# A second level of block products in the second matrix product of a fused block, with its sums on GpSimd and all steps in a table

## The chip, the core and the metric

One NeuronCore of a Trainium2 chip runs the whole program. The metric is device time in microseconds of one execution, as the median of several runs. The engines are TensorE (PE in the profile; PEld is its load of stationary operands), VectorE (DVE), ScalarE (ACT), GpSimd (POOL) and SyncE (SP), which here only issues DMAs.

## The reference

32 sequences of 128 tokens with 512 features go through a conditioned block in float32:

```python
m = mask[:, :, None]
shift, scale, gate_msa = jnp.split(silu(t) @ ada_w + ada_b, 3, axis=1)
norm = jnp.where(m, layernorm(x) * (1 + scale[:, None]) + shift[:, None], 0)
fwd, bwd = two MLPs of width 512 with exact gelu on norm
x = x + gate_msa[:, None] * jnp.where(m, fwd + bwd, 0)
shift_mlp, scale_mlp, gate_mlp = jnp.split(silu(t) @ ffada_w + ffada_b, 3, axis=1)
ff_norm = layernorm(x) * (1 + scale_mlp[:, None]) + shift_mlp[:, None]
h = gelu(ff_norm @ ff_w1 + ff_b1, approximate=True)     # 512 -> 1024
return x + gate_mlp[:, None] * (h @ ff_w2 + ff_b2)      # 1024 -> 512
```

Few tokens are masked in, so the first half is small; what fills the time is the second half: for every token a first product (512 to 1024) and a second one (1024 to 512).

## The kernel before

The first 82 us do the masked tokens and the opening. Then four pairs follow (p = 0 to 3), each of two sides of four sequences, 1024 tokens. A pair's two sides are the two row blocks of a block product after Strassen and Winograd: seven products of half size instead of eight, with sums of blocks before and after.

The first product (FirstProduct) applies this twice, with seven streams of seven phases; one phase is four records of TensorE of 256 columns. Results gather in two PSUM banks, e and a, are copied or added into the hidden tiles ha and hb, and pass through gelu on ScalarE. Sums of hidden blocks run on GpSimd.

The second product (SecondProduct) applies it once. The list ORDER names fourteen steps: products P1 to P7, each for U (the first 256 columns of tokens of both sides) and V (the rest). `step` issues a step: two tiles of 128 tokens, four matmuls each of 256 output columns, with the tokens as stationary operand (`of_batch` takes every second float) and weights of `fw2` or sums of them in `t_2` as moving operand. Each of U and V has its own banks e and a. P3, P7 and P4 come last. After P5 ScalarE keeps a copy p5 of e and seeds e again; VectorE forms sums of hidden blocks (L1266, L1276, L1283, L1341); after a product that completes a block of results, `finish` multiplies it by the gate into a tile t (L1293) and adds that to x (L1295), both on VectorE, and `store` writes x out. The last half step of the last pair goes to two banks of its own (`last`), with a gate, an addition and a store for each.

Beside the second product, the next pair is prepared: its x is normalised and turned in blocks on VectorE (L945, L1490), moved between tiles by 32 DMAs, 24 from SyncE's queue and 8 from ScalarE's (L972), scaled in place by 32 activations on ScalarE (L955), and summed into token blocks s1, s2 and s4 by four VectorE operations (L1002). The loop over `step` puts these in between by hand-written places (`put`). All engines run in the order in which the code records the instructions; nothing is reordered, and an instruction waits for those it depends on.

## Time and profile before

| | us |
|---|---|
| median of 3 runs | 453.68 |
| the runs | 453.67 to 453.86 |
| the profiled execution | 453.94 |
| its span | 452.2 |
| TensorE busy, of the span | 444.6 |
| VectorE, ScalarE, GpSimd busy | 334.8, 179.0, 158.3 |
| span behind the last matmul | 4.65 |

A row of instructions names line, engine, operation, tiles written and read, and their size; then busy time, mean duration in ns, and the idle time of the engine ahead of it with what ended it. One matmul of the code leaves two records on TensorE. A record's mean duration contains its way through the pipeline (379 ns at 256 columns), so the pace is read from rows of the chain or the timeline: length over count. PEclk is the granted clock of TensorE, full from the opening on.

### The profile page before, as it was taken

What the parts mean: (1) busy time and instruction counts of PE and PEld (TensorE: products, weight loads), DVE (VectorE), ACT (ScalarE), POOL (GpSimd) and SP (SyncE); (2) the same over time, 40 slices, a digit from 0 to 9 for tenths busy, and PEclk for the clock granted to TensorE, in tenths of its full rate; (3) what the DMA queues carried; (4) which work ended last, traced back from release to release, by engine and by line L of the source; (5) the groups of instructions that cost most, each with busy time, mean ns of one, the idle gap of its engine ahead of it and who ended that gap; (6) DMA issues with size and microseconds to landing.
All of it is one profiled execution on the core that took longest, in us unless ns stands there. A gap on an engine that the chain in (4) does not pass through costs nothing.

```text
span 452.2 us, 6204 instructions
## 1 busy us (share of the span) xinstructions
PE 444.6 (98%) x2147; PEld 376.1 (83%) x2147; DVE 334.8 (74%) x573; ACT 179.0 (40%) x389; POOL 158.3 (35%) x154
## 2 busy tenths in 40 slices
PE   8999999999999999999999999999999999999995
PEld 3884585688898998888899988888999888899995
DVE  5798798877699677977895779878956785434645
ACT  3124127253651831546528315464274244642000
POOL 4211460089760000797600007977000027560000
PEclk9999999999999999999999999999999999999998
DMA  7999439847335517741275176412751434122022
GB/s 249 375 399 408 171 72 331 290 152 251 107 138 143 93 49 268 234 138 36 94 189 92 46 267 230 141 38 92 187 95 46 175 128 128 36 93 95 0 94 96
DMA packets 56768, 70.84 MB, mean 157 GB/s; under 512 B 34724, under 2 KB 35836, under 8 KB 55710
## 3 DMA queue, kind: packets, MB, share of 16 engines
q1 hardware_dynamic: 43790, 57.76, 39.2%
q0 software_dynamic: 4160, 10.54, 6.6%
q10 hardware_dynamic: 8784, 2.11, 2.5%
q8 instruction: 18, 0.29, 0.2%
q14 instruction: 16, 0.13, 0.1%
HBM read 56.71 MB, written 13.70 MB: 156 GB/s over the span
## 4 chain that ended last, share of the span: by engine, by line
PE 88%; DVE 5%; issue 2%; POOL 2%; DMA 1%; ACT 1%; POOLq 0%; DVEq 0%
PE a_o L1319 21%; PE a_m L1132 20%; PE e_o L1319 16%; PE e_m L1132 15%; PE po_s L222 6%; PE ph_s L681 2%; PE ph_s L205 2%; DVE xn L945 1%; DVE xn L1490 1%; PE pm_ss L308 1%; PE last L1319 1%; PE a_m_alone L1132 1%; DMA x_wide<-t_s 1%; DMA x<-x_wide,slot_i 1%; PE pm_f L308 1%
## 5 line engine op out<-in xcount | busy, mean ns | idle before, releaser
L1183 POOL TENSOR_TENSOR ha<-p_m,ha 128x512 f32<-128x512 f32 x20 | 25.9, 1293 | 176.3 <-ACT ha L1190 166.4
L1319 PE MATMUL e_o<-fw,ha 128*128 128x256 f32 x256 | 57.9, 379 | 1.0 <-DVE ha L1341 1.0
L1319 PEld LDWEIGHTS e_o<-fw,ha 128*128 128x128 f32 x256 | 50.2, 196 | 6.3 <-issue 1.3
L955 ACT ACTIVATE xT<-xT,modT 128x128 f32<-128x128 f32 x112 | 45.0, 496 | 23.9 <-DMA xT<-xn 22.3
L1319 PE MATMUL a_o<-t,hb 128*128 128x256 f32 x240 | 54.1, 379 | 0.0
L1319 PEld LDWEIGHTS a_o<-t,hb 128*128 128x128 f32 x240 | 47.1, 196 | 4.7
L1094 ACT ACTIVATE hb<-hb,biasT 128x256 f32<-128x256 f32 x64 | 29.0, 500 | 28.3 <-POOL hb L1216 16.1
L1146 ACT COPY p_m<-e_m 128x512 f32<-128x512 f32 x27 | 15.9, 587 | 56.4 <-PE e_m L1132 56.4
L901 POOL DMA_INDIRECT x<-x_rows,slot_i x24 | 27.3, 1136 | 6.2 <-issue 5.4
L1183 POOL TENSOR_TENSOR hb<-p_m,hb 128x512 f32<-128x512 f32 x20 | 29.2, 1461 | 0.3
L1319 PE MATMUL e_o<-fw,s 128*128 128x256 f32 x128 | 28.9, 379 | 0.0
L1319 PE MATMUL a_o<-fw,ha 128*128 128x256 f32 x128 | 28.9, 379 | 0.0
L1319 PE MATMUL a_o<-t,s 128*128 128x256 f32 x128 | 28.9, 379 | 0.0
L222 PE MATMUL po_s<-w,h_s 128*128 128x512 f32 x64 | 28.4, 594 | 0.0
L1190 ACT COPY ha<-e_m 128x512 f32<-128x512 f32 x32 | 18.5, 580 | 24.8 <-PE e_m L1132 24.4
L1319 PEld LDWEIGHTS a_o<-fw,ha 128*128 128x128 f32 x128 | 25.1, 196 | 2.5
L1319 PEld LDWEIGHTS e_o<-fw,s 128*128 128x128 f32 x128 | 25.1, 196 | 2.5
L1319 PEld LDWEIGHTS a_o<-t,s 128*128 128x128 f32 x128 | 25.1, 196 | 2.5
L1157 DVE TENSOR_TENSOR e_m<-a_m,ha 128x512 f32<-128x512 f32 x20 | 13.9, 697 | 17.0 <-POOL ha L1183 7.6
L1094 ACT ACTIVATE ha<-e_m,biasT 128x256 f32<-128x256 f32 x48 | 20.1, 469 | 14.4 <-PE e_m L1132 14.4
L1132 PE MATMUL a_m<-xT,tw 128*128 128x256 f32 x96 | 24.7, 380 | 0.0
L1132 PE MATMUL e_m<-s,fw 128*128 128x256 f32 x92 | 23.7, 380 | 0.0
(234 smaller groups left out, 894.7 us busy)
## 6 DMA issues: line engine op xcount, KB each, us to landing
x<-in_x_dram SPq DMA_DIRECT2D x16, 512.0 KB, 7.5
tw<-t_rows SPq DMA_DIRECT2D x16, 512.0 KB, 4.0
gate<-gate_rows POOLq DMA_DIRECT2D x8, 1024.0 KB, 4.9
out_dram<-x SPq DMA_DIRECT2D x15, 512.0 KB, 4.5
tw<-t_rows SPq DMA_DIRECT2D x16, 384.0 KB, 3.6
xT<-xn SPq DMA_DIRECT2D x80, 64.0 KB, 2.2
ada_f<-in_L_cond_ffada_w_dram SPq DMA_DIRECT2D x4, 768.0 KB, 14.9
ada_a<-in_L_cond_ada_w_dram SPq DMA_DIRECT2D x4, 512.0 KB, 3.5
```

Source lines behind the costliest of these rows:

```text
L205: nc.tensor.matmul(ph[:, :n], w[:, k, ts(f, P)], xT[:, k, :], start=(k == 0), stop=(k == KC - 1))
L222: nc.tensor.matmul(po, h[f][:, ts(i, P)], w[:, f, :], start=(f == 0 and seeded is None), stop=(f == HC - 1), skip_group_check=seeded is no ...
L308: nc.tensor.matmul(pm[ts(j, B), : (hi - lo) * P], sT[:, k, :], kinds[:, k, lo:hi, ts(j, P)], start=(k == 0 and not begun), stop=True, skip ...
L901: nc.gpsimd.indirect_dma_start(out=xs[i // G][i % G // 2][:, i % 2], out_offset=None, in_=x1_rows, in_offset=bass.IndirectOffsetOnAxis(ap= ...
L955: nc.scalar.activation(out, src, AF.Identity, bias=shift, scale=scale)
L1094: nc.scalar.activation(dst[:, n], src[:, n], AF.Gelu_apprx_tanh, bias=biasT[:, f : f + 1])
L1132: nc.tensor.matmul(bank[:, ts(n, QT)], self.w_block(j, product)[:, ts(n, P)], self.x_block(j, product), start=(product in ("P1", "P5") and ...
L1146: nc.scalar.copy(p5, e)
L1157: nc.vector.tensor_tensor(e, a, p5, add)
L1183: nc.gpsimd.tensor_tensor(self.place(RESULT[j], c), self.p5[j], other, ALU.add)
L1190: nc.scalar.copy(self.place(RESULT[j], c), src)
L1319: nc.tensor.matmul(part, of_batch(src[:, k], i), w[product][:, k, :], start=(last and k == 0), stop=True, skip_group_check=True,)
```

## The change

The three products P3, P7 and P4 of each second product are no longer done as two steps each, U and V. Each is divided once more (class Inner): seven inner products p1 to p7 of 256 tokens by 256 hidden features by 128 columns. p1, p6 and p7 share one bank (`one`), p5 has another (`five`); ScalarE copies p5, p1 and p7 into a tile d (C in the table), VectorE adds d's part to the bank after p6 and p7 (V), and then adds d to the outer bank (join, J). p2, p3 and p4 go straight into the outer banks. The four sums of token blocks of each (S1 to S4) run on GpSimd. The seven blocks of weights of each product come from `fw2`, `t_2` and twelve sums made by VectorE in pair 0, kept in quarters of the first product's weights that are no longer read and in a small new tile.

Four of the eight results of a pair (both blocks of side 0) are copied out of PSUM by ScalarE and multiplied by the gate and added to x by GpSimd; the other four are multiplied on VectorE in place in PSUM and added. The third block result of P7 is formed in e in place of a tile. The normalising of side 1 moves to ScalarE, with a small operation for its bias. The 32 moves are single steps. And every step of the loop has a name, and a table (ORDER) gives for each pair the sequence of all steps, first product and preparation included.

```diff
+    INNER = ("P3", "P7", "P4")
...
+            if by_vector:
+                nc.vector.tensor_scalar(
+                    t, src, self.mv[:, i, 0:1], self.rstd[:, i : i + 1], ALU.subtract, ALU.mult
+                )
+            else:
+                nc.scalar.activation(
+                    t, src, AF.Identity, bias=self.lift[:, i : i + 1], scale=self.rstd[:, i : i + 1]
+                )
...
-            nc.vector.tensor_tensor(t, view, gate, ALU.mult)
+            nc.vector.tensor_tensor(view, view, gate, ALU.mult)
...
+        def kept(self, c, side, h, n):
+            t = tp.tile([P, 512], F32, tag="t", name=f"t_{self.p}_{c}{side}{h}")
+            self.own[c, side, h] = t
+            nc.scalar.copy(t, self.banks[c][n])
...
+            nc.gpsimd.tensor_tensor(view, view, self.gate[side][:, 2 * c : 2 * c + 2, part], ALU.mult)
...
+            nc.gpsimd.tensor_tensor(xt, view, xt, ALU.add)
...
+        def direct(self, product, q):
+
+            c, n = {"p2": (0, 0), "p3": (0, 1), "p4": (1, 0)}[q]
+            bank = bank_of(product, self.banks[c])
+            out = bank.rearrange("p (i f) -> p i f", i=2)[:, :, ts(n, P)]
+            self.inner[product].multiply(q, out, False)
+
+        def join(self, product, c):
+
+            bank = bank_of(product, self.banks[c]).rearrange("p (i f) -> p i f", i=2)
+            nc.vector.tensor_tensor(bank, bank, self.inner[product].d[:, c], ALU.add)
...
+    class Inner:
...
+        def sum(self, j):
+            if j < 3:
+                self.s[j] = self.second.s_of(self.product, j - 1)
+            (a11, a12), (a21, a22) = self.x
+            s1, s2 = self.s.get(1), self.s.get(2)
+            out, x, y, op = {
+                1: (s1, a21, a22, ALU.add),
+                2: (s2, s1, a11, ALU.subtract),
+                3: (a21, a11, a21, ALU.subtract),
+                4: (a11, a12, s2, ALU.subtract),
+            }[j]
+            nc.gpsimd.tensor_tensor(out, x, y, op)
+
+        def multiply(self, q, out, start, tiles=range(2)):
...
+            w = inner_w[self.product][q]
+            for i in tiles:
+                for k in range(2):
                     nc.tensor.matmul(
-                        part,
+                        out[:, i % out.shape[1]],
                         of_batch(src[:, k], i),
-                        w[product][:, k, :],
-                        start=(last and k == 0),
+                        w[:, k, :],
+                        start=(start and (i == 0 or out.shape[1] == 1) and k == 0),
                         stop=True,
                         skip_group_check=True,
                     )
...
+        def copy(self, q):
+
+            if self.d is None:
+                self.d = self.second.d_of(self.product)
+            c, n, which = {"p5": (1, 1, "five"), "p1": (0, 0, "one"), "p7": (1, 0, "one")}[q]
+            nc.scalar.copy(self.d[:, c, :, ts(n, P)], self.view(which))
+
+        def with_five(self, c):
+
+            five = self.d[:, 1, :, P:]
+            nc.vector.tensor_tensor(self.d[:, c, :, P:], self.view("one"), five, ALU.add)
...
+            c030 4i3 lg1 c010 c031 6i7 c011 V6i7 S4i7 R001 c013
+            n1P1 7i7 K010 J70 3i7 A2 V7i7 2i7 E20 S1i4 5i4 S3i4 C7i7 C5i4 1i4 J71 c023 A3 G110 n1P5
...
+        steps.run(ORDER.get(p, "").split())
```

In the table 6i7 is p6 of P7, V6i7 the addition behind it, S1i4 the sum S1 of P4, C a copy, c a scaling, K, G and R the copy, gate and addition of a result, J a join, A a sum of token blocks, E the third block result, n1P1 a phase of the next pair's first product.

TensorE in pair 1, from P2 of V on. Before, with e and a the banks of U (0) and V (1):

```order
L1319 MATMUL e_o_1_1789<-fw_312,ha_1432 128x256 x8
L1319 MATMUL a_o_1_1790<-t_314,s_1_1505 128x256 x8
L1319 MATMUL e_o_0_1731<-fw_312,ha_1432 128x256 x8
L1319 MATMUL a_o_0_1732<-t_314,hb_1433 128x256 x8
L1319 MATMUL e_o_1_1789<-fw_312,ha_1432 128x256 x8
L1319 MATMUL a_o_1_1790<-t_314,hb_1433 128x256 x8
L1132 MATMUL e_m_1_2023<-s_2_1974,fw_311 128x256 x2
```

And of the change, from the first half of P6 of V on, where one and five are the banks of the inner products and si the sums that GpSimd makes:

```order
L1384 MATMUL a_o_1_1834<-t_314,s_1_1852 128x256 x4
L1470 MATMUL five_P_2033<-fw_312,si_1_P_2024 128x128 x4
L1470 MATMUL one_P_2043<-fw_312,ha_1558 128x128 x4
L1384 MATMUL a_o_1_1834<-t_314,s_1_1852 128x256 x4
L1470 MATMUL one_P_2043<-inner_more,si_1_P_2027 128x128 x4
L1470 MATMUL five_P_2066<-t_314,si_1_P_2048 128x128 x4
L1470 MATMUL one_P_2043<-inner_more,ha_1558 128x128 x4
L1470 MATMUL e_o_0_1800<-fw_312,ha_1558 128x128 x4
L1470 MATMUL one_P_2097<-t_314,hb_1559 128x128 x4
...
L1470 MATMUL e_o_1_1833<-t_313,ha_1558 128x128 x4
L1470 MATMUL one_P_2097<-t_313,si_1_P_2072 128x128 x4
```

Where six steps of eight matmuls stood, inner products of four stand, P3's (one_P_2043) and P7's (one_P_2097) side by side; between the uses of one bank lies one other product, or two.

GpSimd at the same place in pair 1, where before it had no work. L1459 is a sum S, L1346 a gate, L1353 an addition to x:

```order
L1459 TENSOR_TENSOR si_1_P_2024<-ha_1558 128x512
L1459 TENSOR_TENSOR ha_1558<-ha_1558 128x2x256
L1459 TENSOR_TENSOR si_1_P_2027<-si_1_P_2024,ha_1558 128x512
L1459 TENSOR_TENSOR si_1_P_2048<-hb_1559 128x512
L1459 TENSOR_TENSOR ha_1558<-ha_1558,si_1_P_2027 128x2x256
L1459 TENSOR_TENSOR si_1_P_2072<-si_1_P_2048,hb_1559 128x512
L1459 TENSOR_TENSOR hb_1559<-hb_1559 128x2x256
L1346 TENSOR_TENSOR t_100_2021<-t_100_2021,gate_0_1878 128x512
L912 DMA gate_1_2116<-gate_rows 128x2048
L1459 TENSOR_TENSOR hb_1559<-hb_1559,si_1_P_2072 128x2x256
L1353 TENSOR_TENSOR x_1_387<-t_100_2021,x_1_387 128x2x256
L1459 TENSOR_TENSOR si_1_P_2151<-hb_1559 128x512
```

The last row is S1 of P4, the eleventh operation of the engine from P3's S1 on, apart from the gate's issue.

VectorE at the end of the last pair, from P4's p6 on (before, the rows there were four gates and additions and those of `last`). L1502 is V, L1417 a join, L1328 a gate, L1335 an addition, L1425 and L1427 those of `last`:

```order
L1395 TENSOR_TENSOR e_o_1_3110<-a_o_1_3111,p_o_1_3182 128x512
L1328 TENSOR_TENSOR e_o_1_3110<-e_o_1_3110,gate_1_3159 128x512
L1502 TENSOR_TENSOR xn_d_3223<-one_P_3314,xn_d_3223 128x2x128
L1417 TENSOR_TENSOR a_o_0_3077<-a_o_0_3077,xn_d_3223 128x512
L1335 TENSOR_TENSOR x_2316<-e_o_1_3110,x_2316 128x2x256
L1502 TENSOR_TENSOR xn_d_3223<-one_P_3314,xn_d_3223 128x2x128
L1417 TENSOR_TENSOR a_o_1_3111<-a_o_1_3111,xn_d_3223 128x512
L1328 TENSOR_TENSOR a_o_1_3111<-a_o_1_3111,gate_1_3159 128x512
L1328 TENSOR_TENSOR a_o_0_3077<-a_o_0_3077,gate_1_3159 128x512
L1335 TENSOR_TENSOR x_2316<-a_o_1_3111,x_2316 128x2x256
L1335 TENSOR_TENSOR x_2314<-a_o_0_3077,x_2314 128x2x256
L1425 TENSOR_TENSOR last_3371<-last_3371,gate_1_3159 128x128
```

Both V and both joins of P4 stand among the last gates and additions, and the rows of `last` are behind all of them.

More of the change, by code (lines that the diff above doesn't have):

```diff
@@ new lines @@
+        put("E1", second.third, 1)
+        sums("P7")
+        apart("P3", "p7")
+        join("P3", 1)
+        put_scales(1)
+        apart("P7", "p5", "p1")
+        direct("P3", "p2")
+        apart("P7", "p6")
+        join("P7", 0)
+        direct("P3", "p3")
+        second.finish(put, 0, 0, 1, 0)
+        put("o00", second.store, 0, 0)
+        apart("P7", "p7")
+        join("P7", 1)
+        sums("P4")
+        direct("P3", "p4")
+        second.finish(put, 1, 0, 1, 0)
+        put("o10", second.store, 1, 0)
```

829 lines of the change are left out of this document (551 added, 278 removed).

## The prediction

> **What bounds the kernel now.** I read the page's busy shares and chain first, then the windows by stage, then the waits of TensorE.
>
> ```profile
> PE 444.6 (98%) x2147; PEld 376.1 (83%) x2147; DVE 334.8 (74%) x573; ACT 179.0 (40%) x389; POOL 158.3 (35%) x154
> PE 88%; DVE 5%; issue 2%; POOL 2%; DMA 1%; ACT 1%; POOLq 0%; DVEq 0%
> ...
> 82.60:168.08 85.48, 84.50 (x390) 74.66 (x389) 68.47 (x106) 41.46 (x91) 35.91 (x30) 1.00 0.50 155
> 168.08:259.03 90.95, 90.95 (x421) 80.94 (x421) 71.92 (x110) 41.50 (x91) 36.08 (x30) 1.00 0.47 137
> 447.55:452.20 4.65, 0.00 (x0) 0.00 (x0) 0.85 (x2) 0.00 (x0) 0.00 (x0) 0.72 0.25 86
> ...
> PE e_o L1319 <- DVE ha L1341: 1.0, 1, 1.0
> ```
>
> The columns of the window rows are length, then busy time of PE, PEld, DVE, ACT and POOL, then clock and DMA. From 168 us on TensorE is busy without a hole (90.95 of 90.95), at full clock. Its one wait on an engine after the opening is 1.0 us, in pair 0. The rest is a tail of 4.65 us. So only two things can shorten this kernel: less matmul time, or a shorter tail. Whatever makes TensorE wait is paid in full.
>
> **Matmul time.** The chain in order of time and the timeline give the price of a matmul record (each matmul of the code leaves two records).
>
> ```profile
> 74.02 8.59 PE po_s L222 x20
> 154.27 3.45 PE e_o L1319 x16
> 16.57 3.65 PEld L681 LDWEIGHTS ph_s<-xT_s,w 128*128 128x128 f32 x32 [0.35 <-issue]
> ...
> L681 PEld LDWEIGHTS ph_s<-xT_s,w x64: 186/192/192, 16.6 to 25.4; 128*128 128x128 f32 x64
> L1319 PEld LDWEIGHTS a_o<-fw,ha x128: 195/197/197, 122.5 to 409.0; 128*128 128x128 f32 x128
> L1132 PEld LDWEIGHTS a_m<-xT,t 128*128 128x128 f32 x88 | 16.7, 190 | 2.3
> ```
>
> 512 columns take 8.59/20 = 0.4295 us, 256 columns 3.45/16 = 0.2156. On that line 128 columns would take 0.2156 - 0.2139/2 = 0.1087 us. The trace holds a row with 128 columns and new weights at every matmul, L681: from the first load's start to the last one's end 3.65 us, less the last one's own 0.192, over 31 steps, which is 0.1115 us. There the load of weights seems to set the pace. The second product reads its weights with a step of two floats (of_batch), L681 without a step; the loads of L1319 last 196 ns against 190 at L1132, where the step is one. If these 6 ns add to the pace, a record takes 0.1175. I take 0.113, near the row that has the shape, and keep 0.1087 and 0.1175 as ends.
>
> A block product is now two steps of 16 records, 6.90 us. The change makes it 7 inner products of 8 records: 56 x 0.113 = 6.33 us. It saves 0.58 (0.82 at 0.1087, 0.66 at 0.1115, 0.32 at 0.1175). Break-even is 6.90/56 = 0.123. The first three pairs have 9 such products: **-5.2 us** (-7.3 to -2.9). The last pair is counted with the tail.
>
> The Trainium skill, SBUF — State Buffer, section "Door 1: The DMA port swizzle", says that accesses of SBUF keep full bandwidth as long as at least two fall in each 16-byte line, so that four-byte numbers may step by up to four. By that rule the step of two floats costs nothing; the pace would stay 0.1115 and the nine products would save 6.0 us, which puts the forecast below at 450.3. The 196 against 190 ns speaks mildly against it, and no run so far shows the stepped load at 128 columns.
>
> **What must keep up: the sums on GpSimd.** Durations that the new work takes, from groups and timeline:
>
> ```profile
> L1212 POOL TENSOR_TENSOR hb<-hb 128x512 f32<-128x512 f32 x8 | 10.2, 1270 | 0.9 <-DVE hb L1167 0.9
> L912 POOL DMA_DIRECT2D gate<-gate_rows x8 | 4.6, 574 | 10.2 <-PE a_m L1132 10.2
> L1341 DVE TENSOR_TENSOR ha<-ha,s 128x1024 f32<-128x1024 f32 x8 | 9.7, 1218 | 0.0
> L1331 DVE TENSOR_TENSOR t_last<-last,gate 128x256 f32<-128x256 f32 x2 | 0.8, 425 | 1.2 <-PE last L1319 1.2
> L197 ACT COPY xT_s<-ptr_s 128x256 f32<-128x256 f32 x8 | 2.5, 380 | 18.3 <-PE ptr_s L194 18.3
> L1132 PE MATMUL a_m<-xT,t 128*128 128x256 f32 x88 | 22.6, 379 | 0.0
> ...
> 145.75 1.22 DVE L1341 TENSOR_TENSOR ha<-ha,s 128x1024 f32<-128x1024 f32 x1
> 147.11 0.68 PE L1319 MATMUL e_o<-fw,ha 128*128 128x256 f32 x2 [0.97 <-DVE ha L1341]
> ...
> 443.93 3.62 PE L1319 MATMUL last<-t,hb 128*128 128x256 f32 x16
> 445.85 0.42 DVE L1331 TENSOR_TENSOR t_last<-last,gate 128x256 f32<-128x256 f32 x1 [0.31 <-PE last L1319]
> ```
>
> A sum is 1.27 us, a step from VectorE's end to TensorE 0.14 (146.97 to 147.11), a step from TensorE to VectorE 0.2 (the first half of `last` is issued by 443.93 + 8 x 0.2156 = 445.65). Take pair 1 and count from the end of P2's second half. VectorE's last sum on ha (1.22) ends at 1.4, so GpSimd starts P3's S1 at 1.5 and TensorE, which has 3.45 us of P6 first, can start P3's p5 at 3.45: S1 is ready at 2.8. The order of GpSimd puts S1 of P4 eleventh of the 1.27-us operations, behind one gate issue (0.57): 1.5 + 11 x 1.27 + 0.57 = 16.0. TensorE reaches P4's p5 after 13 inner products of 8 x 0.113 = 0.904, half of P6 (1.73) and one first-product phase (0.86): 3.45 + 11.75 + 2.59 = 17.8. S2 of P4 is ready at 18.6 and wanted at 20.5. Slack of 1.8 and 1.9 us: hidden. Gate multiplication and addition on GpSimd (8 x 1.27 a pair) come in between or behind, and only stores and later loads of x wait for them. So GpSimd's 12 + 8 operations, 25 us a pair, cost nothing if the slack holds.
>
> **What must keep up: the hand-offs.** Four inner products share one PSUM bank: p1, ScalarE copies it, p6 adds, VectorE reads (V), p7 adds, both read, and only then may the next block product's p1 start. Where V lies between two uses TensorE has one inner product in between (0.90 us) and needs 0.2 + 0.42 + 0.14 = 0.76. That fits with 0.14 to spare if VectorE is free; an operation of 0.6 or 1.2 us in its way makes TensorE wait. There are four such places in a pair (before P3's p7, P7's p1, P7's p7, P4's p7). The copies (0.38) have two and more products as cover. I allow 0.1 us for each place and a little for the rest: 0.5 us a pair, **+1.5 us** for three (0 to 5).
>
> ScalarE's copies also stand behind scalings that wait for the moves of xn to xT. Those rows:
>
> ```profile
> xT<-xn SPq DMA_DIRECT2D x80, 64.0 KB, 2.2
> ...
> 227.00 16.93 SPq L972 DMA_DIRECT2D xT<-xn  x24
> 238.31 3.45 PE e_o L1319 x16
> 246.06 6.39 ACT L955 ACTIVATE xT<-xT,modT 128x128 f32<-128x128 f32 x16 [2.10 <-DMA xT<-xn]
> ```
>
> In pair 1 SyncE needs 16.93 us to issue 24 moves, and the second side lands at 246.06, 4.3 us after P2 ended (241.76). The table lists the first move ahead of nine half steps of 1.73 and one phase of 0.86 that end with P2, so it starts about 16.4 us before P2's end, against 14.8 now; the last move, 16.93 of issue and 2.2 of landing later, is there 2.7 us after P2. ScalarE's copies that p6 of P3 needs stand ahead of the scalings of that side, and P7's wait for ten of them (0.4 apart): they are done near 10.4 and wanted at 10.6. Hidden, barely. Moving the normalising of side 1 to ScalarE and half of the finishing off VectorE frees 4 x 0.6 + 8 x 0.6 us of VectorE a pair; V and the joins put 6 x 0.4 + 6 x 0.6 back: no change on the path. The twelve sums of weights (about 5 us of VectorE, pair 0 alone) fall where VectorE is fullest, so I leave pair 0's stall of 1.35 us (1.22 us of L1341 and its step) where it is.
>
> **The tail.** In the last pair no first product follows. The rows of before:
>
> ```profile
> 419.92 3.45 PE e_o L1319 x16
> 433.77 0.69 DVE L1349 TENSOR_TENSOR c_o<-a_o,p_o 128x512 f32<-128x512 f32 x1 [2.04 <-PE a_o L1319]
> 434.49 0.69 DVE L1293 TENSOR_TENSOR t_o<-c_o,gate 128x512 f32<-128x512 f32 x1
> 442.12 0.69 DVE L1295 TENSOR_TENSOR x<-x,t_o 128x512 f32<-128x512 f32 x1
> 442.74 0.68 DVE L1293 TENSOR_TENSOR t_o<-a_o,gate 128x512 f32<-128x512 f32 x1
> 448.04 0.42 DVE L1333 TENSOR_TENSOR x<-x,t_last 128x256 f32<-128x256 f32 x1
> ```
>
> P2 ends at 423.37, VectorE at 448.46, the span at 452.20: 28.85 us in all, 3.74 of them after VectorE. Dependent VectorE operations start 0.72 apart (433.77, 434.49), independent ones 0.62 (442.12, 442.74). After the change, with time 0 at the end of P2 and half of P6 still to come: TensorE has 3.45 + 1.73 + 16 x 0.904 = 19.64 up to P4's p6, which ends at 20.55. From there VectorE is full: the third block result of the second half at 19.85, its gate, V at 21.2, so p7 starts at 21.77, not 20.55; join, addition, V at 22.9, join 23.3, gates 24.05 and 24.7 (p2 ends at 24.5), additions 25.3 and 25.9, and four operations of 128 columns of about 0.35 from 26.5: 27.95. With 3.74 behind it the end is at 31.7; less the 1.73 of P6 that had been done before, 29.95 against 28.85: **+1.1 us** (0.5 to 2). The last pair thus gives its own matmul saving away and a little more.
>
> **Sum.** -5.2 + 1.5 + 1.1 = -2.6. The profiled execution took 453.94 us (span 452.2): 451.3; it lies 0.26 above the median of 453.68, so **451.1 us**.
>
> **Rivals.**
> *A, all hidden.* The load hides completely (0.1087) and the table removes pair 0's stall and the waits of hand-offs: -7.3 - 1.35 + 0.8 = -7.9, **445.8**. For it: 1.8 us of slack at GpSimd. Against: L681 shows 0.1115 even without the step.
> *B, the hand-offs are not covered (slower).* Sixteen places with 0.14 us to spare, VectorE near three quarters busy there; an operation of 0.62 in its way costs 0.48. If that happens at every place: 16 x 0.47 = 7.5, -5.2 + 7.5 + 1.1 = +3.4, **457.1**. It decides from a mean of 0.26 us a place (4.1/16). For it: no stretch of before has TensorE wait for two engines within two microseconds. Against: VectorE has gaps there.
> *C, GpSimd and VectorE block each other.* Rows:
>
> ```profile
> 217.55 1.74 POOL L1183 TENSOR_TENSOR hb<-p_m,hb 128x512 f32<-128x512 f32 x1
> 217.48 0.68 DVE L1266 TENSOR_TENSOR s<-hb 128x512 f32<-128x512 f32 x1
> 219.22 1.57 DVE L945 TENSOR_SCALAR xn<-x,mv,rstd 128x512 f32<-128x512 f32 x1
> 221.47 0.52 DVE L945 TENSOR_SCALAR xn<-x,mv,rstd 128x512 f32<-128x512 f32 x1
> ```
>
> A GpSimd sum beside such VectorE work took 1.74 instead of 1.27, a VectorE operation beside a GpSimd sum 1.57 instead of 0.52. The change puts GpSimd's sums beside VectorE's four 1.22-us sums of token blocks. Two of them fall before P4's S1: 2 x 1.22 - 1.8 = 0.6 us late; the fourth, held up by 1.05, feeds the next product with about 0.4 of slack: 0.65. That is 1.3 us a pair, 3.9 for three in place of 1.5: -5.2 + 3.9 + 1.1 = -0.2, **453.5**. The Trainium skill states it as a rule, SBUF — State Buffer, section "Who interferes with whom": a VectorE instruction with two inputs in SBUF contends with a GpSimd instruction that reads SBUF, and the later one blocks fully. By that rule C is what happens; the rows above agree in kind. I give it little because the two engines meet there only if both run as early as counted. The gates and additions of the change read PSUM on VectorE, which the rule leaves free.
>
> **Chances.** Forecast 0.53, A 0.15, B 0.20, C 0.12. This kernel's measurement tells about 0.2% (0.9 us) from no change. Faster by more: A and 0.50 of the forecast, 0.65; within: 0.03 of the forecast and 0.11 of C, 0.14; slower: B and 0.01, 0.21. The forecast's own range is 449 to 453; to leave out no more than two in ten the range is 446 to 456.5.
>
> **What would show it.** Groups of the new matmul line: busy over count 0.11 to 0.118 us; 0.123 or more refutes the saving. Waits of TensorE: under 0.3 us at each hand-off; B shows as many waits of 0.4 to 1 us on VectorE in the second product. Mean of a GpSimd sum in the inner stretch: near 1.27; C shows 1.6 and more, and TensorE waiting for GpSimd at P4. Tail: last matmul to span's end about 7 us against 4.65. Wrong altogether if TensorE waits for ScalarE's copies: then the moves of xn came late.

## The result: 470.2 us against 453.7, and the profile after

The changed kernel takes 470.18 us as the median of four executions (466.1 in the profiled one, 469.8, 470.6 and 474.0 in the others), the kernel before 453.73 us beside it. The slow execution of 474.0 us is left out of the ratio, which is 1.033, with a 95% interval of 1.027 to 1.040: **slower by 3.3%**, where 0.6% faster was forecast. The kernel before repeats within 0.04% here and within 0.6% beside the later experiments; the changed one does not repeat even so well, and the reason turns out to be part of the result.

The page of the changed kernel: busy time of each engine, and the shares of the chain that ended last.

```profile
PE 443.4 (95%) x2435; PEld 379.7 (82%) x2435; DVE 348.1 (75%) x592; ACT 206.6 (44%) x453; POOL 266.5 (57%) x234
PE 65%; DMA 15%; DVE 9%; POOL 5%; issue 3%; SPq 2%; ACT 0%; POOLq 0%; ACTq 0%; DVEq 0%
```

TensorE's busy time hardly fell (444.6 to 443.4 us) though 288 more records are there. GpSimd's rose from 158.3 to 266.5 us. The chain, which was 88% TensorE, now runs through DMA, VectorE and GpSimd for 29% of the span (8% before). The waits of TensorE (total, times, longest, in us), where before had a single one of 1.0 us after the opening:

```profile
PE e_m L1152 <- DVE e_m L1172: 3.8, 2, 3.4
PE a_m L1152 <- DVE e_m L1185: 3.1, 2, 2.1
PE one_P L1470 <- DVE xn_d L1502: 3.0, 2, 2.0
PE e_o L1384 <- ACT e_o L1304: 0.7, 1, 0.7
PE one_P L1470 <- ACT xn_d L1497: 0.5, 1, 0.5
```

They sum to 11.1 us, and most lie not at the inner products but in the first product (`e_m`, `a_m`, L1152), which the change left as it was and only re-ordered. In time: 3.4 us at 110 (pair 0), 2.0 at 161 (pair 0, first inner products), 1.0 and 0.4 at 202 and 205 (pair 1), 2.1 at 294, 0.7 at 333 and 0.5 at 345 (pair 2), 1.1 at 451 (last pair). Measured from record to record each is 0.1 to 0.2 us longer; the expectations below use those lengths (3.5, 2.1, 1.1, 0.6, 2.3, 0.9, 0.6, 1.2), the text uses those of the view.

**The ledger** of the profiled executions, 466.11 against 453.94, +12.2 us. Matmuls: 672 records at 0.1178 (inner products of eight records that follow each other without a wait start 0.942 apart) in place of twelve products of 6.90, 79.2 - 82.8 = -3.6. Waits: 11.1 - 1.0 = +10.1. Tail from the last matmul's end to the span's end: 464.36 - 456.52 = 7.84 against 4.68, +3.2. The rest, 2.5 us, is in restarts and in steps too short for the waits view. In other executions about 4 us more come on top; the experiment without gathers shows what probably makes them.

### The profile page after: what moved, and what is told of

Read it like the earlier page. It is cut to its first block, busy times and chain, and to the rows that moved or that the text cites. A ratio compares the mean times of both kernels' runs of the same rounds, so it can differ in the third digit from the quotient of the medians.

```text
span 464.4 us, 7016 instructions
## 1 busy us (share of the span) xinstructions
PE 443.4 (95%) x2435; PEld 379.7 (82%) x2435; DVE 348.1 (75%) x592; ACT 206.6 (44%) x453; POOL 266.5 (57%) x234
## 4 chain that ended last, share of the span: by engine, by line
PE 65%; DMA 15%; DVE 9%; POOL 5%; issue 3%; SPq 2%; ACT 0%; POOLq 0%; ACTq 0%; DVEq 0%
PE a_m L1152 13%; PE e_o L1384 11%; PE a_o L1384 10%; PE e_m L1152 10%; PE one_P L1470 7%; PE a_o L1470 4%; DMA fw<-in_L_cond_ff_w_dram 3%; DMA x<-in_x_dram 3%; PE po_s L222 3%; DMA w<-in_L_cond_bwd_w_dram 3%; PE e_o L1470 2%; DMA out_dram<-x 2%; PE five_P L1470 2%; SPq L988 2%; POOL x L901 1%
## 5 line engine op out<-in xcount | busy, mean ns | idle before, releaser
L965 ACT ACTIVATE xT<-xT,modT 128x128 f32<-128x128 f32 x112 | 47.4, 500 | 12.9 <-DMA xT<-xn 12.9
L1346 POOL TENSOR_TENSOR t<-t,gate 128x512 f32<-128x512 f32 x16 | 21.3, 1337 | 42.3 <-ACT t L1340 42.3
L1204 DVE TENSOR_TENSOR hb<-a_m,hb 128x512 f32<-128x512 f32 x40 | 27.2, 682 | 15.1 <-PE a_m L1152 13.5
L901 POOL DMA_INDIRECT x<-x_rows,slot_i x24 | 27.0, 1123 | 14.8 <-DMA x<-in_x_dram 8.8
L1502 DVE TENSOR_TENSOR xn_d<-one_P,xn_d 128x256 f32<-128x256 f32 x24 | 10.1, 421 | 27.1 <-PE one_P L1470 22.4
L1384 PE MATMUL a_o<-fw,ha 128*128 128x256 f32 x128 | 29.9, 379 | 0.0
L1384 PE MATMUL e_o<-fw,ha 128*128 128x256 f32 x128 | 29.2, 380 | 0.7 <-ACT e_o L1304 0.7
L1384 PEld LDWEIGHTS e_o<-fw,ha 128*128 128x128 f32 x128 | 25.1, 196 | 3.6 <-ACT e_o L1304 1.1
L1152 PE MATMUL a_m<-xT,tw 128*128 128x256 f32 x96 | 24.5, 381 | 0.1
L1152 PE MATMUL e_m<-s,fw 128*128 128x256 f32 x92 | 23.7, 380 | 0.0
```

Of the source, the lines that this page charges most:

```text
L901: nc.gpsimd.indirect_dma_start(out=xs[i // G][i % G // 2][:, i % 2], out_offset=None, in_=x1_rows, in_offset=bass.IndirectOffsetOnAxis(ap= ...
L965: nc.scalar.activation(out, src, AF.Identity, bias=shift, scale=scale)
L1152: nc.tensor.matmul(bank[:, ts(n, QT)], self.w_block(j, product)[:, ts(n, P)], self.x_block(j, product), start=(product in ("P1", "P5") and ...
L1204: nc.vector.tensor_tensor(dst, a, other, ALU.add)
L1346: nc.gpsimd.tensor_tensor(view, view, self.gate[side][:, 2 * c : 2 * c + 2, part], ALU.mult)
L1384: nc.tensor.matmul(bank[:, ts(i, D // 2)], of_batch(src[:, k], i), w[:, k, :], start=False, stop=True, skip_group_check=True,)
```

## The experiments

### 1. Without the weight sums

The longest wait starts here. VectorE and GpSimd in the timeline of the changed kernel (start, length, engine, line, operation), and TensorE's restart:

```profile
104.75 1.02 POOL L901 DMA_INDIRECT x<-x_rows,slot_i  x1 [0.16 <-issue]
105.51 5.51 DVE L1826 TENSOR_TENSOR inner_more<-fw 128x256 f32<-128x256 f32 x1
105.81 1.27 POOL L1213 TENSOR_TENSOR ha<-ha 128x512 f32<-128x512 f32 x1
107.03 1.27 POOL L1179 TENSOR_TENSOR ha<-p_m,ha 128x512 f32<-128x512 f32 x1
108.26 1.26 POOL L1179 TENSOR_TENSOR hb<-p_m,hb 128x512 f32<-128x512 f32 x1
109.47 1.25 POOL L1213 TENSOR_TENSOR ha<-ha 128x512 f32<-128x512 f32 x1
113.30 0.92 PE L1152 MATMUL e_m<-xT,fw 128*128 128x256 f32 x3 [3.35 <-DVE e_m L1172]
```

A sum of weights (L1826), 0.41 us where GpSimd leaves it alone (at 165.57 us, say), takes 5.51: as long as GpSimd's four sums stand back to back. It ends 0.3 us after the last of them, and the seed that TensorE needs (L1172) stands behind it in VectorE's order. Beside the sums of the first inner products the same operation takes 1.5 us each, four times in a row, and TensorE waits 2.0 us at 161:

```profile
157.24 1.45 POOL L1459 TENSOR_TENSOR si_P<-hb 128x512 f32<-128x512 f32 x1
157.48 1.50 DVE L1826 TENSOR_TENSOR fw<-t,t 128x256 f32<-128x256 f32 x1
158.65 1.47 POOL L1459 TENSOR_TENSOR ha<-ha,si_P 128x512 f32<-128x512 f32 x1
158.90 1.50 DVE L1826 TENSOR_TENSOR t<-fw,inner_more 128x256 f32<-128x256 f32 x1
```

First theory: the weight sums are the cause.

```diff
-            nc.vector.tensor_tensor(o, x, y, ALU.subtract)     # combine_inner
+            return
```

> The changed kernel without the twelve sums of weights on VectorE in pair 0 (the inner products read existing weight blocks instead, so the values differ). Theory L (in pair 0 a VectorE sum with both inputs in SBUF is held for whole GpSimd sums): the stalls of TensorE at 109.6 us (3.5 us) and 160.6 us (2.1 us) go, the profiled time falls from 466.1 to about 460.5, and the three executions lie closer together than 466 to 474. Rival H (GpSimd has too much work of its own, the 12 sums and 8 gate operations of a pair, and VectorE's weight sums only happen to stand there): both stalls stay within 0.5 us of what they were and the time stays at 465 or more. Under both, the stalls at 202 to 205 and at 294 us (4.0 us) stay.

Measured: 472.0 us, profiled 467.6. The wait at 161 us is gone; the one at 110 is not, it grew to 3.9 us. The next operation with two inputs in SBUF took the place of the victim:

```profile
108.56 6.10 DVE L1291 TENSOR_TENSOR s<-hb 128x512 f32<-128x512 f32 x1
```

So the weight sums explain 2.0 us; for the rest the theory in this form falls. What stays is the dense run of GpSimd sums.

### 2. The step of the stationary operand

```diff
-                        of_batch(src[:, k], i),      # Inner.multiply: every second number
+                        src[:, k, ts(i, P)],         # 128 neighbours
```

> The changed kernel with the stationary operand of the inner products read as 128 neighbouring numbers instead of every second one (the tokens come out in another order, so the values differ). Theory W (the step of two sets the pace): records of the inner products start 111.5 ns apart as at the opening's 128-column matmuls, not 117.7; 672 records give 4.2 us, profiled time near 462. Rival (the width or the second operand sets it): 117 to 118 ns again and no change in time beyond the spread of the changed kernel.

A stretch of sixteen records of the inner products in the chain of waits, first in the changed kernel, then here:

```profile
169.96 1.88 PE a_o L1470 x16
```

```profile
170.15 1.79 PE a_o L1470 x16
```

1.88/16 = 0.1175 us, 1.79/16 = 0.1119 us: the step costs 6 ns a record, as the longer loads had suggested. Yet the time was 473.2 us. TensorE came earlier to hand-offs that were late anyway: its wait for L1185 rose from 3.1 to 7.1 us, and three of its waits were followed by half the clock (0.50 from 162, 207 and 302 us on, for about 3.4 us each; the next experiment says when that happens). The gain is real and cannot be seen until those are gone (experiment 14).

### 3. Without the gathers of pairs 2 and 3

The chain of waits of the changed kernel in pair 1:

```profile
181.84 4.99 DMA out_dram<-x
186.84 7.18 DMA x<-in_x_dram
...
197.72 1.24 POOL x L901
...
201.58 1.29 POOL ha L1179
...
205.33 0.71 DVE e_m L1172
```

A store lands, the load into its buffer follows, GpSimd's gathers wait for the load, and the sum that VectorE's seed (L1172) needs stands behind the gathers in GpSimd's order. SyncE's issues of the kernel before, then of the changed one, show that it starts with the stores:

```profile
168.93 0.39 SPq L1299 DMA_DIRECT2D out_dram<-x  x1
170.82 1.90 SPq L412 DMA_DIRECT2D x<-in_x_dram  x2
```

```profile
180.71 2.08 SPq L1366 DMA_DIRECT2D out_dram<-x  x3
186.29 0.94 SPq L412 DMA_DIRECT2D x<-in_x_dram  x2
```

The first store comes 12 us later and the loads 15. Of these, 4.4 us are pair 0's longer waits (3.35 + 1.98 against 0.97).

```diff
-            if p < NP:      # gathers(w, n, p, which)
+            if p < 2:
```

> The changed kernel without GpSimd's gathers of x rows for pairs 2 and 3 (masked tokens there keep other values). Theory X (GpSimd's finishing makes the stores late, the loads of the next x wait for them, and the gathers at the head of GpSimd's queue hold back its sums): the stalls of TensorE at 202.3 and 205.3 us and at 294.3 us, 1.14 + 0.6 + 2.3 us, go below 0.3 us each, although the stores and loads stay as late; profiled time near 462, and the waits of GpSimd for x landing are gone. Rival H (GpSimd's amount of work): GpSimd's first sums of stream 6 in pair 1 still start after 200 us and at least half of the stalls stays. Under both the pair 0 stalls stay (5.6 us).

Measured: 464.4 us, profiled 464.7. The waits at 202, 205 and 294 us are gone (4.0 us from record to record), so the gathers carry them. The profiled time should have been 462; the other 2.7 us are something new. TensorE waited at 110 us exactly as before, 3.36 us against 3.35:

```profile
113.28 2.07 PE L1152 MATMUL e_m<-xT,fw 128*128 128x256 f32 x4 [3.36 <-DVE e_m L1172]
```

But then it ran at half clock for 6 us. Windows (length, busy time of PE, PEld, DVE, ACT and POOL, granted clock, DMA) of this run and of the changed kernel:

```profile
113.30:119.30 6.00, 6.00 (x14) 4.83 (x15) 5.58 (x10) 0.84 (x2) 5.01 (x3) 0.51 0.00 0
```

```profile
113.30:119.30 6.00, 6.00 (x28) 5.09 (x29) 5.93 (x11) 1.92 (x4) 5.32 (x4) 1.00 0.21 66
```

14 records in place of 28 in the same 6 us. The Trainium skill, TensorE: Matmul & The Clock Gate, Part 1, says that the clock is halved after an idle window of about 3.4 us and that this window runs freely, so that the same gap may or may not fill one. The traces agree on the window and not on how idle it must be, and the measurement decides. In each of the twenty traces every change of the clock behind 84 us (but for the end of the kernel) lies on a grid of 3.41 us. In 39 of the grid's stretches with full clock TensorE was idle for 57% or more, and half the clock follows on all 39; in the other 2128 it was idle for 56% or less, and on none does it follow. The gap of 3.35 us fell into two such stretches in the changed kernel (44% and 54% of them) and filled 72% of one here. A single wait of 1.95 us was enough where it fell into one stretch (experiment 9 at 163 us), and one of 3.77 us had no effect where it was cut (experiment 13's second kernel at 149 us).

This is probably why the changed kernel's times lie apart (466.1 at a mean clock of 0.995, 469.8 and 470.6 at 0.984): its profiled execution was the lucky one. The traces of the others are not there to show it.

### 4. The rest of the change without the inner products

```diff
-            for q in qs:                         # apart
-                inner[product].steps(put, q)
+            return
...
-                put(f"{q[1]}i{product[1]}", second.direct, product, q)
+                if q != "p2":
+                    multiply(product, q == "p4") # the whole block product again
```

The sums of weights go with the inner products, and the last pair ends without the split of its last quarter.

> The changed kernel with its order table, its halves finished by GpSimd, its normalising on ScalarE and its gating in PSUM, but with the last three block products multiplied whole as before (no inner products, no sums for them on GpSimd or VectorE). Theory L and X together: matmul time goes back up by 3.7 us (12 x 0.31), the pair 0 stalls (5.6 us) go with the weight sums, the tail shrinks from 7.8 to about 5 us, the stalls at 202 and 294 us stay in part because the stores stay late (2 to 4 us): 456 to 459. Rival (the inner products are what costs, all else is free): at or below 453.9, all stalls gone. Second rival (the rest of the change costs most): above 460.

Measured: 472.6 us, as slow as with them. The two longest waits:

```profile
PE e_m L1152 <- DVE s L1018: 4.8, 1, 4.8
PE e_m L1152 <- DVE e_m L1172: 4.3, 2, 3.9
```

The second is the dense run again (here F00, 6.09 us, is the victim). The first is new: in pair 2 the scalings on ScalarE wait 9.8 us for moved rows of xn, and the token blocks behind them come late. So the rest of the change is enough to make the kernel slow; that the inner products add nothing of their own is not shown by it, since their places in the table stay empty here.

### 5. Victims moved out of the dense run

```diff
-  0: ... 6e 5P4 w30 x17 ... 7P1 F00 3P2 ... z00 7P7 ... K000 w31 ...
+  0: ... 6e 5P4 x17 ... 7P1 3P2 ... z00 F00 7P7 ... K000 w30 w31 ...
```

> The changed kernel with two entries of pair 0's table moved: VectorE's first sum of the second product (F00) behind the first normalising, and the first sum of weights (w30) ahead of the second. Theory L2 (a run of GpSimd sums without a hole between them holds back whatever VectorE operation with both inputs in SBUF comes up in it: a weight sum in the changed kernel, F00 where the weight sums are left out): no VectorE operation takes over 2.5 us between 100 and 120 us, the stall at 109.6 us (3.5 us) goes, the profiled time is near 462.6 with a clock of 0.995 or more, and the executions lie within 3 us, because no stall of over 3 us is left to halve the clock. Rival L3 (the run always finds a next victim, the weight combination of 1024 columns at 116 us): a stall of 2 us or more stays between 105 and 122 us and the time at 465 or more.

Measured: 469.4 us, profiled 468.7. The wait at 110 us is gone, and one of 2.3 us stands at 115: the rival. The wait at 294 us rose from 2.1 to 3.5 us, with half the clock behind it. The third victim, passed by three GpSimd sums:

```profile
111.22 5.24 DVE L403 TENSOR_TENSOR t<-fw 128x1024 f32<-128x1024 f32 x1
```

### 6 to 8. Three repairs of the table, one on the other

Three gathers behind the first sums of stream 6 (the tables of pairs 1 and 2 likewise):

```diff
-  0: ... nx23 ... nx25 ... nx24 ...
+  1: ... 6w22 x23 ... 3w12 x24 ... 3w22 x25 ...
```

> As the run before, and in pairs 1 and 2 three of the six gathers that stood ahead of GpSimd's first sums of stream 6 stand behind them. Theory X: the stalls at 202, 205 and 294 us (1.1 + 0.6 + 2.3 us) go below 0.5 us together, profiled time 458.7, no stall over 2.5 us left, executions within 2 us. Rival (GpSimd has too much work there, so that the sums behind are late instead): the stalls move by a few us and at least 2 us of the 4 stay.

Measured: 470.9 us. The waits at 202 and 205 us went to one of 0.9; in pair 2 one of 3.2 us stands at 301 in place of that at 294 (3.5 in experiment 5): VectorE's statistics now wait for the gathers, with TensorE's seed (L1172) behind them.

```profile
301.00 0.69 DVE L934 BATCH_NORM_STATS2 st<-x 128x6 f32<-128x512 f32 x1 [3.47 <-DMA x<-x_rows,slot_i]
```

Ten weight sums on GpSimd:

```diff
-            nc.vector.tensor_tensor(o, x, y, ALU.subtract)
+            engine.tensor_tensor(o, x, y, ALU.subtract)      # GpSimd but for w70 and w71
```

> As the run before, and ten of the twelve weight sums of pair 0 are made by GpSimd, which stood idle from 134 to 147 us, instead of VectorE. Theory L: VectorE has no operation of 128x256 in SBUF beside GpSimd's sums at 156 to 161 us, the stall at 160.6 us (2.1 us) goes, profiled time 456.6. Rival (GpSimd's sums of the first inner product now come too late): a stall of 2 us or more before the first inner products, time not under 458.5.

Measured: 473.7 us (471.8 to 474.4, and 515.5 at a mean clock of 0.85 in one execution, whose cause isn't known). The wait for VectorE at 161 us went, and TensorE waited for GpSimd instead: the sum of P3 came 3.3 us late.

```profile
PE five_P L1470 <- POOL si_P L1459: 3.3, 1, 3.3
```

Pair 2:

```diff
-  2: ... P5V0 ... P1V0 ... P2V0 ... P2V1 ... P6U1 ... 1i3 ... C1i3 ... C5i3
+  2: ... P1V0 P5V0 ... P6U1 P2V0 ... P2V1 ... 1i3 C5i3 C1i3 ...
```

> As the run before, and in pair 2 one half step of P1 and one of P6 are moved ahead so that ScalarE's seed has cover, and two copies of ScalarE stand ahead of the scalings that wait for moved rows. Theory: the stalls at 333.1 us (0.9 us) and 344.6 us (0.6 us) go, profiled time 455.1. Rival (the moves of rows themselves are late, whatever stands ahead of them): the second stall stays or grows behind the copies and the time is within 0.5 us of the run before.

Measured: 474.9 us. The wait for the seed at 333 us fell to 0.3; in place of that for a copy at 345 there are two for GpSimd's sums, 1.0 us each, which neither the theory nor its rival had named. Three repairs, and each ended its wait and made the next.

### 9. The halves finished by VectorE again

```diff
-    APART = ((0, 0, 0), (1, 0, 0), (0, 0, 1), (1, 0, 1),)
+    APART = ()
```

> The changed kernel, with the halves that GpSimd finishes in pairs 0 to 2 finished by VectorE in PSUM where ScalarE made the copy (eight GpSimd operations a pair less). Theory X (the finishing on GpSimd makes stores, loads and gathers late): out stores of pairs 0 and 1 start 3 us or more earlier, the stalls at 202 to 205 us and at 294 us (1.7 and 2.3 us) go below 0.5 us each, the pair 0 stall at 109.6 us stays; profiled time near 462. Rival (VectorE has no room for these operations in the second product): new waits of TensorE on VectorE of 2 us or more a pair there, time at 466 or more.

Measured: 481.5 us, 11 more: the rival. GpSimd's finishing, which I had suspected, helps: VectorE has no room. New waits for it:

```profile
PE a_o L1384 <- DVE s L1308: 2.1, 1, 2.1
PE e_o L1384 <- DVE ha L1321: 1.7, 1, 1.7
```

The first stores still came at 179.2 us (180.7 in the changed kernel), with 2.2 us more of waits ahead of them; the waits at 202 and 294 us grew to 3.6 and 2.4. So the engine that finishes is not what makes most of the stores' lateness. The chain in experiment 3 starts with a store that waits for VectorE behind the inner products that end at 180.17 us, which points to the order of the products; no run changed that order alone.

### 10 and 11. All known victims moved; and with experiment 9

```diff
-  0: ... w30 ... F00 ... w20 ... G000 ... R000 S1i3 S3i3 ... S2i3 ...
+  0: ... 7e w20 ... z00 F00 ... w30 w31 ... S1i3 S3i3 ... S2i3 G000 R000 ...
```

> The changed kernel with pair 0's table alone edited: the weight combination w20, the first sum F00 and the weight sum w30 stand where GpSimd has holes (behind 7e, z00 and ahead of w31), and GpSimd's first two finishing operations stand behind the sums of the first inner product. Theory L2 (starvation in GpSimd's dense run at 105 to 116 us): with none of the three victims in it, no VectorE operation takes over 2.5 us before 130 us, no stall of over 1 us before 150 us, and the stall at 160.6 us falls from 2.1 to under 1 us: 461, executions within 3 us. Rival L3 (GpSimd's run is late whatever stands on VectorE): a stall of 2 us or more in 105 to 130 us again.

> Both edits of the two runs before together. If the two causes are separate and add: 457, with stalls of under 4 us in all (in pair 2 and at 451 us), clock 0.995 or more in every execution, spread under 1 us. If GpSimd and VectorE simply have too much to do between them, the waits reappear elsewhere and the time is above 461.

Measured: 469.0 and 483.8 us. In the first, the waits before 130 us fell from 3.4 to 1.5 us, the one at 161 from 2.0 to 0.2 with one of 1.5 for GpSimd ahead of it: the theory in part. But one wait of 1.1 us stayed at 124, a fourth victim was found, this one of 4 columns, passed by two sums, and TensorE, now earlier, waited 3.6 us at 201 for the gathers and fell to half clock there. The second, where 457 was expected if the two causes add, is as slow as experiment 9 alone.

```profile
113.60 2.93 DVE L939 TENSOR_SCALAR ve<-mv 128x4 f32<-128x4 f32 x1
```

### 12. A probe in the kernel before

```diff
+        if p == 0:
+            put(4, 4, nc.vector.tensor_tensor, probe, fw1[:, 0, :QT], fw1[:, 1, :QT], ALU.add)
```

> The kernel before, with one extra VectorE operation in pair 0: a sum of two 128x256 blocks of SBUF into an unused tile, 0.42 us by itself, placed in VectorE's order at 108.8 us, where GpSimd has two sums back to back (108.78 to 111.28 us). If a VectorE operation with both inputs in SBUF waits until GpSimd's queue has a hole: it takes about 2.9 us, TensorE's seed that comes next is 1.6 us late, and the time is 1.2 to 1.8 us above before. If it waits for one GpSimd operation at most: 1.7 us, a stall of 0.4 us or less, time within 0.5 us of before.

> The kernel before with the same extra VectorE sum of two 128x256 blocks, now ready at 107.9 us, half way through a GpSimd sum (107.4 to 108.65) behind which another stands (108.6 to 109.9) that needs nothing from VectorE; the one after that waits for VectorE. If such an operation is passed by every GpSimd sum that is ready: it takes about 2.4 us (until 109.9 and 0.4 more). If it gets in at the first change of operations, as the first probe did after 1.5 us: 1.2 us. In both cases a stall of TensorE of at most 1 us.

(The second has it at (4, 2).) Measured: 453.92 and 453.33 us, ratios 1.0007 (0.9993 to 1.0022) and 0.9999 (0.9986 to 1.0011). Both got in at the first change of GpSimd's operations, after 1.52 and 1.10 us. The second came up at 107.30 us, earlier than meant:

```profile
106.86 1.26 POOL L1183 TENSOR_TENSOR hb<-p_m,hb 128x512 f32<-128x512 f32 x1
107.30 1.10 DVE L1450 TENSOR_TENSOR probe<-fw 128x256 f32<-128x256 f32 x1
108.08 1.46 POOL L1212 TENSOR_TENSOR ha<-ha 128x512 f32<-128x512 f32 x1
```

The starvation wasn't reproduced: readiness of the next sum alone does not decide. A count over all twenty traces, behind 82 us, gives a pattern. It takes VectorE's operations of the kinds that are held anywhere, where they came up while GpSimd ran one operation with another right behind it. Of 176 that came up more than 0.8 us before the end of the running one, none was passed by the next; both probes are among these (the second had 107.30 against 108.12). Of 143 that came up 0.4 to 0.8 us before it 13 were passed, of 148 in the last 0.4 us 33. The sixteen that were passed by two to four in a row had come up 0.26 to 0.67 us before an end. That is a pattern, not a test of it; a probe that comes up late was not run.

### 13. The order of the program's code instead of the table

```diff
-        steps.run(ORDER.get(p, "").split())
+        steps.run([])
```

> The changed kernel with its four order tables left empty: every engine's steps stand as the program's code puts them down. Theory T (the table makes the loss: it pulls VectorE's sums into GpSimd's dense run and the rest up against each other): the pair 0 stall at 105 to 115 us is gone as in the kernel before and the time falls below 463. Rival G (the added work of GpSimd and ScalarE makes the loss, in any order): 468 or more, with stalls at the inner products.

> The changed kernel without the inner products (last three block products whole) and with empty order tables, against the same with its tables (472.6). Theory T: within 4 us of the kernel before, 454 to 458, since this order is nearly that of the kernel before. Rival G: the copies, the finishing on GpSimd and the normalising on ScalarE cost by themselves: 462 or more.

Measured: 571.6 and 484.8 us. The table is not what makes the loss: both times the rival. Without it the change costs 100 us more. With the inner products TensorE waits for GpSimd's sums and for VectorE's operation on ha, without them for VectorE:

```profile
PE five_P L1470 <- POOL si_P L1459: 23.7, 8, 4.6
PE e_o L1384 <- DVE ha L1321: 16.7, 4, 9.0
```

```profile
PE e_o L1384 <- DVE ha L1321: 9.7, 3, 4.5
PE a_m L1152 <- DVE hb L1204: 8.0, 3, 3.6
```

The second kernel holds nothing of the change but the copies, the GpSimd finishing, the ScalarE normalising, the gating in PSUM and the single moves, in the order of the program's code, and costs 31 us; the table takes 12 of them back (experiment 4). How much is the code's order and how much each of these parts wasn't separated further.

### 14. The causes taken out together

Experiment 10 with the gathers (3) and the weight sums (1) left out, and then also without the step (2).

```diff
+  edits of experiments 1, 3 and 10
+  edits of experiments 1, 2, 3 and 10
```

> The changed kernel with three causes taken out together: the three victims moved out of GpSimd's dense run in pair 0, no sums of weights, no gathers for pairs 2 and 3. By the sums of the single runs: 466.1 less 3.5 (109 us, of which 1.8 come back at 118 and 124 us) less 2.1 (161 us) less 4.0 (202, 205, 294 us) = 458.3, clock 0.995 or more and executions within 1.5 us, as no stall of over 2.5 us is left. Left over the kernel before: the tail (3 us), the stalls at 333, 345 and 451 us (2.7 us) and 1.8 us in pair 0. If the waits only move on when a cause is taken out: 462 or more.

> The run with three causes taken out (460.1 profiled), and the stationary operand of the inner products read without a step (the tokens come out in another order). If the step costs 6 ns for each of the 672 records: 4.1 us less, 456.0, still 2 us above the kernel before because of the tail and the stalls in pairs 0, 2 and 3. If the shorter products only make the next hand-off late: 458 or more.

Measured: 459.9 us (459.4 to 461.5; profiled 460.1, 458.3 expected) and 457.0 us (456.7 to 457.1; profiled 456.9, 456.0 expected). Both leave work out and compute other values, so they show causes and are not kernels to use. Now most of the causes add, 6.0 of the 7.8 us expected in the first, and with the long stalls most of the spread is gone. Pair 1 of the first of them is as full as before the change (90.95 of 90.95 there):

```profile
168.00:259.00 91.00, 90.97 (x497) 82.61 (x497) 70.00 (x111) 49.07 (x110) 55.46 (x44) 1.00 0.46 133
```

The step is worth 3.2 us of the 4.1 expected; the rest went to the seed and the copies of pair 2, whose waits rose from 1.2 to 2.6 us together. Even so the kernel is 0.7% above before (1.0073, 1.0047 to 1.0098): what is left is the tail (8.2 us) and the waits of pairs 0, 2 and 3.

### 15. The kernel before, one swap

```diff
-                self.finish(c, 0, 0, e)
                 nc.vector.tensor_tensor(ha[:, hh:, tok], ha[:, hh:, tok], s1[c], ALU.subtract)
+                self.finish(c, 0, 0, e)          # in pair 0
```

> The kernel before, with one swap in pair 0: VectorE subtracts the fourth block's input (the 1.22 us operation at 145.75 us that TensorE waits for) ahead of gating and adding the result of P2, not behind. The only stall of TensorE after the opening, 1.1 us at 145.8 us, goes: 452.4 to 452.8. If the gate multiplication is late next (its bank is wanted by the next sum): a stall of 0.5 us or more stays and the time is 453.1 or more.

Measured: 452.45 us, ratio 0.9979 (0.9961 to 0.9998). The last wait of TensorE after the opening is gone:

```profile
PE 444.4 (99%) x2147; PEld 376.4 (83%) x2147; DVE 334.8 (74%) x573; ACT 179.1 (40%) x389; POOL 158.0 (35%) x154
```

A swap of two steps beats both kernels, though by 0.2%, with an interval that only just leaves out no change.

## Why the prediction was wrong, point by point

Of the 14.8 us between the forecast for the profiled execution (451.3) and the measured 466.1, pair 0's waits are 4.4, the chain through stores and gathers 3.5, the price of a record 2.5, the last pair 2.4 and the hand-offs -0.3; the rest of about 2.3 was not placed.

**What bounds the kernel** was right: TensorE had no hole, so every wait is paid in full. The forecast then let 25 us of GpSimd work a pair "cost nothing if the slack holds" and looked for waits at the inner products alone. They came where the old code shares engines with the new.

**Matmul time** (-5.2 for nine products): mis-sized. 0.1175 us was the end of the range and is what it takes; 9 x (6.90 - 56 x 0.1178) = -2.7. By the rule of the Trainium skill cited there (SBUF — State Buffer, section "Door 1: The DMA port swizzle") the step of two would be free; for this load it is not, and the measurement decides: experiment 2 shows 0.1175 with the step and 0.1119 without. Break-even at 0.123 was right, and near.

**Sums on GpSimd** ("slack of 1.8 and 1.9 us: hidden"): right as far as it went. TensorE waits for no GpSimd sum in the changed kernel. But not all sums are near 1.27 us in the inner stretch, as this sign had asked; from 168 to 350 us two kinds of the eight are well above, the others at 1.27 to 1.29:

```profile
L1459 POOL TENSOR_TENSOR hb<-hb 128x512 f32<-128x512 f32 x4 | 6.9, 1713 | 0.2
L1459 POOL TENSOR_TENSOR hb<-hb,si_P 128x512 f32<-128x512 f32 x3 | 5.4, 1804 | 1.6 <-PE one_P L1470 1.6
```

**"Only stores and later loads of x wait for them"**: this step failed first. The first stores are 12 us late; loads, gathers, GpSimd's sums, VectorE's seeds and TensorE follow in one chain, and the chain costs 3.5 us (4.0 from record to record; experiment 3). The lateness was mis-told too: it is for the most part not GpSimd's finishing, which experiment 9 shows to be a help. 4.4 of the 12 us are pair 0's waits, at most 3.7 the finishing (experiment 9: stores 1.5 us earlier with 2.2 us more of waits ahead), and the order of the products is the likely rest (not tested alone).

**"About 5 us of VectorE ... I leave pair 0's stall of 1.35 us where it is"**: failed. The old stall went, and 3.4 + 2.0 us came. 2.0 are the weight sums beside GpSimd's sums (experiment 1). 3.4 are a VectorE operation held for GpSimd's dense run, whichever comes up there (experiments 1, 4, 5, 10).

**Rival C** had the mechanism, both engines blocking each other, but in pair 1, for one operation at a time (1.05 us), and with a chance of 0.12. Missing was that one held operation holds VectorE's whole order, with TensorE's seed in it.

**Hand-offs** (+1.5) were sized about right: waits for V or the copies at the inner products are 1.1 us in the last pair and 0.5 in pair 2. **B** did not happen. **ScalarE's copies** ("hidden, barely"): not in pair 2, where TensorE waits 0.5 us for a copy with moved rows late, as named. The 0.7 us ahead of it are another thing: a seed that ScalarE copies (L1304) as soon as TensorE has made its source, with too little other work for TensorE in between.

**The tail** (+1.1): mis-sized. P2 of the last pair is this piece of the chain, ending at 430.26:

```profile
426.81 3.45 PE e_o L1384 x16
```

From there to the span's end (464.36) it took 34.1 us where 31.7 were counted, which makes +3.5 in the forecast's own terms: 21 inner products at 0.942 instead of 0.904 are 0.8, and 3.74 us behind VectorE became 5.5. The two last stores are issued after the two before them, until 460.35, 1.5 us after VectorE's end (458.88):

```profile
458.38 1.97 SPq L1428 DMA_DIRECT2D out_dram<-x  x2
458.59 0.29 DVE L1427 TENSOR_TENSOR x<-last,x 128x128 f32<-128x128 f32 x1
```

**The clock** appears in no term. With waits of 2 us or more it must: the median lies 16.5 us above before, the profiled execution 12.2.

## What to carry to other kernels

When one engine has no hole, work moved to idle engines is not free: ask of each moved operation which in-order queue it stands in, and what the bound engine needs that stands behind it. Count the saving against its own break-even first: here twelve products could give 3.6 us, and one stall takes as much. A wait of TensorE of about 2 us or more must be costed with the slow clock behind it. Whether it comes depends on where the wait falls on the clock's grid, so a kernel with such waits scatters from execution to execution.

## What the runs showed of the hardware

A VectorE operation with two inputs in SBUF, and also one of 4 columns with one input (L939), was held for up to four GpSimd sums in a row (2.9 to 6.1 us), and by one only in other places. The Trainium skill, SBUF — State Buffer, section "Who interferes with whom", says that whoever issues first holds the shared ports for the whole instruction and the other blocks. The first half agrees; but in the run at 105.5 us VectorE's operation stood waiting before the second, third and fourth sum began, and these went first. When it gets in seems to depend on how late in GpSimd's running operation it comes up (0.8 us before its end was always enough), and on holes after that; why is open.

TensorE's clock was halved, for 3.41 us or a multiple of it, behind every full-clock stretch of its 3.41 us grid in which TensorE was idle for 57% or more, and behind no other (39 of 2167 stretches, experiment 3). After the same gap of 3.35 us it was therefore 1.00 in one execution and 0.51 for 6 us in another.
